# A count moved into the recurrence's bank, and chunk 13's second norm split around chunk 14's last up stages

## The chip, the cores and the metric

The kernel runs on one core of one Trainium2 chip. The metric is the device time of the whole program in microseconds (us). The engines are called PE (TensorE: matrix products), DVE (VectorE), ACT (ScalarE), POOL (GpSimd) and SP (SyncE, here only a queue that issues transfers). Each engine works through its own list of instructions; semaphores tie the lists together. PSUM is the memory into which PE writes its products; a tile of it that is needed again has first to be read by the engine that takes it over.

## The reference

The input x has 2 sequences of 4096 rows of 256 numbers. Two layers follow, each with a residual and a norm:

```
u = x @ W_in + b_in;  g = sigmoid(x @ W_gate + b_gate)
h_t = tanh(h_{t-1} @ A + u_t @ Bm)              # state of 64, step by step
y_t = g_t * (h_t @ C.T + u_t @ D.T) + (1 - g_t) * x_t
x = layernorm(x + (y @ W_out + b_out + x))
...
bw = mean(|w|, per row) * sign(w)               # for w1 (1024 x 256) and w2 (256 x 1024)
x = layernorm(x + gelu(x @ bw1.T + b1) @ bw2.T + b2)
```

## The kernel before

**The recurrence in segments.** Each sequence is cut into 64 segments of 64 steps, and all 128 segments run side by side. A run-in of 48 steps from a zero state gives each segment a guess of its first state. At the end `compare` (four DVE operations, L166 to L172) counts the states for which this guess agreed with what the segment before ended in, into `cnt`. `count` (L175) sums `cnt` over the partitions with a product by ones and copies the sum to `flag` (DVE, L178). All engines load the flag at L864; where some state was not met, a branch recomputes everything one segment after another. In the runs shown the branch is not taken.

**Chunks.** The 8192 rows are 16 chunks of 512 (`Chunk`, numbers 0 to 15; `end` is 15). A chunk's life is a row of small steps:

- `mix`, `mix_end`, `project(0)`, `project(1)`: the gated output and its product with W_out (PE, L400). At the end of `project(1)` DVE adds the residual (L411), which gives `x1`. `stats1`, `shift`, `norm` are the first layer norm.
- `turn` (for the chunks 0, 1 and 15) or `blocks` (the others): the transposed x1. It is split into a part `hi` rounded to the reduced type fp32r, and a rest `lo`, so that two products make up for one of full width. For `turn` these are L439 (ACT) and L441 (DVE), for `blocks` they are `split_hi` (ACT, L464) and `split_lo` (DVE, L468).
- `up(g)`, g = 0 to 3: two tiles of 128 hidden units. Each is four products of 128x512 (PE, L487) into a bank, and a GELU on ACT (L497) which reads the bank. After the second tile ACT rounds both to `hhi` (L506). `low(g)` is the rest `hlo` on DVE (L513).
- `down(g)`: sixteen products of 128x256 (PE, L529), hhi and hlo of two hidden tiles for four blocks of rows. At the end of `down(3)` DVE scales the sums out of PSUM (`scale`, L545).
- `rest` adds the bias b2 on POOL (L360), `add` the scaled sums to x1 on DVE (L551).
- `stats` is the second norm's statistics: on DVE `bn_stats` (L256), `bn_aggr` (L260) and the variance plus epsilon (L265), then its power -1/2 on POOL (L266). `store` follows: the shift `nm_b` on DVE (L271), four scalings on ACT (L279), and one transfer to the output, issued by SP (L566).

**Banks.** Up tiles, gates and, before the change, the count take PSUM tiles from a pool `p_1` of three banks with one tag, "h". `p_h` (L149) is a bank of its own, in which the recurrence's steps put their products. `mix`, `project` and `turn` share the pool `p_m`, the down sums have `p_2`; both have one tile.

**Order.** Nothing is reordered by a scheduler: the main part is one block with a manual schedule, and each engine gets its instructions in the order in which the program emits them. The loop over c at L778 staggers the chunks: turn c holds up(c), down(c - 1, 2) and down(c - 1, 3), then the end of chunk c - 1 (add, stats, store), down(c, 0) and down(c, 1), and the early steps of the chunks c + 1 and c + 2. The recurrence's steps are spread over the loop by costs and are over before turn 14. The change concerns turns 13 and 14; the numbers in what follows are chunk numbers, so low(14,1) is `low(1)` of chunk 14. In turn 14 the program emits before the change: up(14,0), low(13,3), the first norm of chunk 15, down(13,2), low(14,0), half of compare, up(14,1), down(13,3) with its scaling, turn(15), low(14,1), the other half of compare, add(13), stats(13), rest(15), up(14,2), low(14,2), store(13), down(14,0), up(14,3), down(14,1). After the loop follow the count, up(15,0), low(14,3), low(15,0), down(14,2), down(14,3), and the rest of chunks 14 and 15 (L843 to L860).

Of the kernel before, what the change touches and what calls it, by code (L numbers as in the profile page):

```python
# [8 lines left out]
FP = mybir.dt.float32  # L9
# [7 lines left out]
P = 128  # L17
# [6 lines left out]
N = 512  # L24
# [3 lines left out]
TB = N // P  # L28
# [9 lines left out]
def gated_recurrence_then_binary_ffn(  # L38
# [16 lines left out]
    nc = tc.nc  # L55
# [7 lines left out]
    p_1 = ctx.enter_context(tc.tile_pool(name="p_1", bufs=3, space=PSUM))  # L63
# [27 lines left out]
    ones = cp.tile([P, P], FP, name="ones")  # L91
    neg_half = cp.tile([P, TB], FP, name="neg_half")
    cnt = cp.tile([P, 2], FP, name="cnt")
    flag = cp.tile([1, 1], I32, name="flag")
# [54 lines left out]
    p_h = p_s.tile([P, W], FP, name="ps_s")  # L149
# [23 lines left out]
        yield  # L173

    def count():  # L175
        ps = p_1.tile([P, N], FP, tag="h", name="ps_cnt")
        nc.tensor.matmul(ps[0:1, 0:1], ones[:, 0:1], cnt[:, 0:1], start=True, stop=True)
        nc.vector.tensor_copy(flag, ps[0:1, 0:1])  # L178


    def load_weights():
# [148 lines left out]
    class Chunk:  # L330
# [218 lines left out]
        def add(self, blocks=range(TB), engine=nc.vector):  # L549
            cut = slice(blocks[0], blocks[-1] + 1)  # L550
            engine.tensor_tensor(  # L551
                self.x1[:, cut, :], self.x1[:, cut, :], self.o[:, cut, :], ALU.add
            )
            yield
# [88 lines left out]
    plan = [*range(L - WARM, L), *range(L)]  # L643
    done = 0
# [3 lines left out]
    def ready():  # L648
        return done < len(plan) and plan[done] // SPC in have_u

    def next_steps():
        nonlocal done
        steps(plan[done])
        done += 1
        if done == WARM:
            first_states()
        for i in range(3):
            if done == WARM + (i + 1) * SPC:
                ch[i].load_h()
        if waiting and not held:  # L660
            for what, args in waiting:
                what(*args)
            waiting.clear()
# [10 lines left out]
    def step():  # L674
        if ready():
            next_steps()

    def do(i, what, *args, pace=5600):
        if not 0 <= i < len(ch):
            return  # L680
        if what == "load":
            need = WARM + (ch[i].c + 1) * SPC
            while done < need:
                next_steps()
            ch[i].load_u()
            ch[i].load_h()
        elif what in ("load_n", "load_x", "load_gate_x"):
            getattr(ch[i], what)()
        else:
            emit(what, getattr(ch[i], what)(*args), pace)  # L690
# [7 lines left out]
    with tc.manual_schedule(engines={ET.PE, ET.Activation, ET.DVE, ET.Pool, ET.SP}):  # L698
        waiting = []
        for c in range(FIRST + 1, FIRST + 6):  # L700
            load_xT(c)
        idle_products(7)
        emit("u", u_of_chunks(FIRST), 1 << 30)
        since = 0
        pairs = [(5, 6), (7, 8), (9, 10), (11, 12), (13, 14), (), (1, 2)]
        loads = [[10, 11], [12, 13], [14, 15, 0], [1, 2], [3], [], []]
        for n, pair in enumerate(pairs):
            before = 2 if n == 0 else 1
            parts(before, EARLY)
            if pair:  # L710
                emit("", u_of_chunks(*pair))
                if pair == (13, 14):
                    emit("", u_of_chunks(15, 0))
                emit("u", [None], EARLY)
            for c in loads[n]:
                load_xT(c)
            if n == 0:
                load_weights()
            if n == 3:
                halve_weights()  # L720
            if n >= 5:
                load_xT(n + 3)
                ch[n - 4].load_n()
                if n == 5:
                    ch[0].load_u()
                else:
                    ch[0].load_n()
                    ch[1].load_u()
                    ch[2].load_u()
            for i in range(7 - before):  # L730
                if 1 <= n < 5 and i == 0:
                    load_w(n - 1)
                if 2 <= n < 6 and i == 3:
                    prepare_w(n - 2)
                parts(1 if (n, i) != (6, 5) else 0, EARLY)
        assert done >= WARM + SPC, done
        emit("u", u_of_chunks(3), EARLY)
        for i in range(4):
            ch[i].xt = x_tiles[i]
        ch[0].in_x = ch[1].in_x = True  # L740
        parts(1, 600)
        do(0, "mix", pace=850)
        do(0, "mix_end")
        held = True
        parts(2, 600)
        assert done >= WARM + 2 * SPC, done
        do(1, "mix", pace=850)
        do(1, "mix_end")
        held = False
        do(0, "project", 0, p_2, "o", pace=1700)  # L750
        do(0, "project", 1, pace=1700)
        do(0, "stats1")
        assert done >= WARM + 3 * SPC, done
        do(2, "mix", pace=1700)
        do(0, "shift")
        do(1, "project", 0, p_2, "o", pace=1700)
        do(0, "norm")
        do(1, "project", 1, pace=1700)
        do(1, "stats1")
        parts(1, 1700)  # L760
        while waiting:
            next_steps()
        waiting = None
        do(0, "turn", True)
        emit("", mean_w2())
        mixed = ch[2].mix_end()
        next(mixed)
        do(1, "norm", nc.vector)
        do(0, "rest")
        next(mixed)  # L770
        parts(2, 1700)
        for i in (4, 5):
            do(i, "load_x")
        end = len(ch) - 1
        parts_met = compare()
        since = -1 << 40
        late = gates(ch[10:], TB)
        for c in range(end):  # L778
            far = 0 < c < end - 1
            if far:  # L780
                do(c + 1, "shift")
                do(c + 1, "norm")
                do(c - 1, "low", 3)
                do(c + 1, "blocks")
            do(c, "up", 0)
            if c == end - 1:
                do(c - 1, "low", 3)
                do(c + 1, "shift")
                do(c + 1, "norm")
            step()  # L790
            do(c - 1, "down", 2)
            if c > 0:
                do(c + 2, "mix")
            do(c, "low", 0)
            mixed = ch[c + 2].mix_end() if 0 < c < end - 1 else iter(())
            next(mixed, None)
            if c == end - 1:
                assert done == len(plan), done
                next(parts_met)
                next(parts_met)  # L800
            do(c + 3, "load")
            do(c + 6, "load_x")
            if c % 2 == 0:
                do(10 + c // 2, "load_gate_x")
            do(c, "up", 1)
            step()
            do(c - 1, "down", 3)
            next(mixed, None)

            def add():  # L810
                do(c - 1, "add")
                do(c - 1, "stats")

            if 1 <= c <= 12:
                add()
                emit("gate", (next(late, None) for _ in range(KD)))
            if not far:
                do(c + 1, "turn")
            do(c, "low", 1)
            if c == end - 1:  # L820
                assert done == len(plan), done
                next(parts_met)
                next(parts_met)
            if not 1 <= c <= 12:
                add()
            do(c + 1, "rest")
            do(c, "up", 2)
            step()
            if far:
                do(c + 1, "split_hi")  # L830
            do(c, "low", 2)
            do(c - 1, "store", range(TB), nc.scalar)
            do(c + 3, "load_n")
            do(c, "down", 0)
            do(c + 2, "project", 0)
            do(c + 2, "project", 1)
            if far:
                do(c + 1, "split_lo")
            do(c + 2, "stats1")
            do(c, "up", 3)  # L840
            step()
            do(c, "down", 1)
        count()  # L843
        do(end, "up", 0)
        do(end - 1, "low", 3)
        do(end, "low", 0)
        do(end - 1, "down", 2)
        do(end - 1, "down", 3)
        do(end, "up", 1)
        do(end - 1, "add")  # L850
        do(end - 1, "stats")
        do(end, "low", 1)
        do(end, "up", 2)
        do(end, "low", 2)
        do(end, "down", 0, True)
        do(end, "up", 3, True)
        do(end - 1, "store", range(TB), nc.scalar)
        do(end, "low", 3, True)
        do(end, "down", 1)
        do(end, "down_end")  # L860
# [64 lines left out]
```

## Time and profile before

| what | value |
|---|---|
| median of 3 runs | 445.03 us (444.57 to 445.47) |
| time of the profiled execution | 445.99 us |
| span of its instructions | 444.1 us |
| mean granted PE clock in it | 0.985 of full speed |
| PE busy | 428.2 us |
| DVE, ACT, POOL busy | 332.6, 285.5, 153.3 us |
| HBM read, written | 31.43 MB, 8.39 MB |

All times in the text are counted from the start of the profiled span. In a timeline row the columns are start, length in us, engine, line of the kernel, operation, output<-input, shape and count; a bracket gives the idle time of the engine before the row and what ended it. A row of several instructions gives the length from the first start to the last end. In a row of waits the three numbers are total us, times and the longest. PEclk is the granted clock of PE; in the page's row of 40 slices it stands in tenths and 9 means 0.9 or more.

### The profile page before, as it was taken

The numbers are of one execution on the slowest core, as the hardware profiler recorded it, in microseconds if no ns is written. First come the engines' busy times: TensorE is split into PE (matmuls) and PEld (weight loads), VectorE is DVE, ScalarE is ACT, GpSimd is POOL, SyncE is SP. The second block draws the span as 40 slices with busy tenths as digits, with TensorE's granted clock in tenths as the row PEclk, the third lists the DMA queues.
The fourth block names the chain that finished last, engine by engine and source line by source line (L and its number), as shares of the span: only waits on it lengthen the run. The fifth ranks groups of instructions, "written<-read, shape, count | busy, mean of one in ns | idle before, by whom it ended". The sixth has DMA issues, their size and how long they took to land.

```text
span 444.1 us, 6819 instructions
## 1 busy us (share of the span) xinstructions
PE 428.2 (96%) x2402; PEld 346.8 (78%) x2402; DVE 332.6 (75%) x569; ACT 285.5 (64%) x480; POOL 153.3 (35%) x176
## 2 busy tenths in 40 slices
PE   8999999999999999999999999999999999998792
PEld 5665767788888888888888888888887888887781
DVE  0245927986879797969696979797979797977274
ACT  2443452577585958595868676867776768585681
POOL 1000040654342345243523452346252446351213
PEclk9999999999999999999999999999999999999697
DMA  8977614400242524262426251625251323210102
GB/s 299 305 272 261 245 35 131 154 1 7 63 149 57 206 57 154 50 211 55 159 48 216 46 168 43 217 49 169 44 170 42 125 45 121 46 52 0 47 1 100
DMA packets 31479, 51.34 MB, mean 116 GB/s; under 512 B 5328, under 2 KB 19664, under 8 KB 31440
## 3 DMA queue, kind: packets, MB, share of 16 engines
q1 hardware_dynamic: 30864, 50.48, 35.5%
q8 instruction: 21, 0.34, 0.3%
q10 hardware_dynamic: 576, 0.37, 0.3%
q14 instruction: 18, 0.15, 0.1%
HBM read 31.43 MB, written 8.39 MB: 90 GB/s over the span
## 4 chain that ended last, share of the span: by engine, by line
PE 84%; DVE 6%; ACT 4%; DMA 1%; POOL 1%; issue 1%; SPq 0%; POOLq 0%; DVEq 0%
PE ps_h L487 23%; PE ps_o L529 23%; PE ps_g L314 12%; PE ps_z L400 11%; PE ps_y L375 6%; PE ps_s L157 6%; PE ps_u L131 3%; ACT xn L279 2%; DMA xt<-in_xT 1%; ACT h L497 1%; DVE hlo L513 1%; POOL rs_b L266 1%; DVE bs_b L256 1%; ACT hhi L506 1%; DVE xlo L441 1%
## 5 line engine op out<-in xcount | busy, mean ns | idle before, releaser
L529 PE MATMUL ps_o<-sg,hhi 128*128 128x256 f32 x496 | 123.2, 288 | 0.0
L529 PE MATMUL ps_o<-sg,hlo 128*128 128x256 f32 x496 | 119.6, 281 | 0.1
L497 ACT ACTIVATE h<-ps_h,bias_c,al 128x512 f32<-128x512 f32 x128 | 95.2, 771 | 19.4 <-PE ps_h L487 16.1
L487 PE MATMUL ps_h<-xhi,sg 128*128 128x512 f32 x256 | 93.4, 446 | 4.4 <-DVE flag L178 2.9
L529 PEld LDWEIGHTS ps_o<-sg,hhi 128*128 128x128 f32 x496 | 95.0, 192 | 1.0 <-DVE o L545 0.2
L529 PEld LDWEIGHTS ps_o<-sg,hlo 128*128 128x128 f32 x496 | 94.8, 191 | 1.1 <-DVE hlo L513 0.3
L513 DVE TENSOR_TENSOR hlo<-h,hhi 128x1024 fp32r<-128x1024 f32 (+1 forms) x65 | 80.2, 1251 | 9.0 <-ACT hhi L506 9.0
L360 POOL TENSOR_TENSOR xn<-xn,bo_r 128x256 f32<-128x256 f32 x64 | 52.8, 856 | 90.2 <-DMA xn<-in_x 78.7
L487 PE MATMUL ps_h<-xlo,sg 128*128 128x512 f32 x256 | 80.5, 395 | 0.9 <-DVE xlo L468 0.8
L266 POOL TENSOR_TENSOR rs_b<-rs_b,neg_half 128x4 f32<-128x4 f32 (+1 forms) x17 | 29.0, 1703 | 125.8 <-DVE rs_b L265 125.7
L506 ACT CAST hhi<-h 128x1024 fp32r<-128x1024 f32 (+1 forms) x65 | 67.4, 1039 | 2.0
L314 PE MATMUL ps_g<-xt,w_gate 128*128 128x384 f32 (+3 forms) x208 | 66.2, 430 | 0.2 <-DMA w_gate<-in_W_gate 0.2
L487 PEld LDWEIGHTS ps_h<-xhi,sg 128*128 128x128 f32 x256 | 46.6, 190 | 23.1 <-issue 11.7
L158 ACT ACTIVATE st<-ps_s 64x128 f32<-64x128 f32 x112 | 29.9, 267 | 45.9 <-PE ps_s L157 45.5
L487 PEld LDWEIGHTS ps_h<-xlo,sg 128*128 128x128 f32 x256 | 48.3, 189 | 12.7 <-DVE xlo L468 1.2
L157 PEld LDWEIGHTS ps_s<-st,wab 128*128 128x128 f32 x224 | 38.5, 189 | 21.6 <-ACT st L158 9.6
L360 POOL TENSOR_TENSOR xn<-xn,b_r 128x256 f32<-128x256 f32 x64 | 52.3, 848 | 1.1 <-PE ps_t L431 1.1
L400 PE MATMUL ps_z<-w_out,tg 128*128 128x256 f32 x224 | 50.6, 379 | 0.0
L400 PEld LDWEIGHTS ps_z<-w_out,tg 128*128 128x128 f32 x224 | 41.4, 190 | 5.1
L157 PE MATMUL ps_s<-st,wab 128*128 128x128 f32 x224 | 43.8, 277 | 0.1
L279 ACT ACTIVATE xn<-xn,nm_a,rs_a 128x256 f32<-128x256 f32 x60 | 31.2, 591 | 14.4 <-DVE nm_a L271 14.4
L279 ACT ACTIVATE xn<-xn,nm_b,rs_b 128x256 f32<-128x256 f32 x62 | 32.3, 591 | 10.4 <-DVE nm_b L271 10.4
(79 smaller groups left out, 464.6 us busy)
## 6 DMA issues: line engine op xcount, KB each, us to landing
xt<-in_xT SPq DMA_DIRECT2D x35, 512.0 KB, 4.7
xn<-in_x SPq DMA_DIRECT2D x16, 512.0 KB, 3.3
out_y<-xn SPq DMA_DIRECT2D x15, 512.0 KB, 2.6
xlo<-xb SPq DMA_DIRECT2D x208, 32.0 KB, 1.9
hu<-st SPq DMA_DIRECT2D x32, 128.0 KB, 2.3
w1t<-in_w1T SPq DMA_DIRECT2D x2, 512.0 KB, 4.9
w1n<-in_w SPq DMA_DIRECT2D x2, 512.0 KB, 6.7
w2t<-in_w2T SPq DMA_DIRECT2D x2, 512.0 KB, 5.7
```

The costliest lines, as they stand in the source:

```text
L157: nc.tensor.matmul(p_h, ab, st[:, j].rearrange("p b k -> p (b k)"), start=True, stop=True)
L158: nc.scalar.activation(h_of[:, j + 1].rearrange("p b k -> p (b k)"), p_h[TOP, :], AF.Tanh)
L266: nc.gpsimd.tensor_tensor(rs, rs, neg_half[:, cut], ALU.pow)
L279: nc.scalar.activation(r, r, AF.Identity, bias=self.sh[:, i : i + 1], scale=rs)
L314: nc.tensor.matmul(ps[:, cut], w_gate[:, k, bass.ts(m, P)], xt_[:, k, cut], start=k == 0 and i == 0, stop=k == KD - 1, skip_group_check=True,)
L360: nc.gpsimd.tensor_tensor(r[:, i, :], r[:, i, :], row, ALU.add)
L400: nc.tensor.matmul(self.ps_z[:, i, :], self.y[:, k, bass.ts(i, P)], w_out[:, k, :], start=k == 0, stop=k == KD - 1,)
L487: nc.tensor.matmul(ps, sg1[:, k, bass.ts(j, P)], part[:, k, :], start=n == 0, stop=n == 2 * KD - 1,)
L497: nc.scalar.activation(to, ps.rearrange("p (a i c) -> p a i c", a=P // 32, c=32) if self.far else ps, AF.Gelu, bias=b1_c[:, j : j + 1], sc ...
L506: nc.scalar.copy(hi[:, part, :], h[:, part, :])
L513: nc.vector.tensor_sub(lo[:, i, :], h[:, i, :], hi[:, i, :].bitcast(FP))
L529: nc.tensor.matmul(ps[:, i, :], part[:, j % 2, bass.ts(tb, P)], sg2[:, j, :], start=j == 0 and part is self.h[j // 2][0] and first, stop=j ...
```

## The change

In `count` the product of the count goes into the recurrence's bank `p_h`, and no tile of the pool is taken. In turn 14 (c = end - 1) add(13) moves ahead of turn(15), right behind the scaling; stats(13) comes behind low(14,1), ahead of the second half of compare, which was ahead of it; store(13), with its shift, its four scalings and its transfer, moves from behind low(14,2) to behind up(14,3). In turn 13 (c = end - 2) split_lo(14) moves from behind project(15,1) to between project(15,0) and project(15,1). For all other turns the new conditions give the old order. An assertion of the program's construction goes.

```
     def count():
-        ps = p_1.tile([P, N], FP, tag="h", name="ps_cnt")
-        nc.tensor.matmul(ps[0:1, 0:1], ones[:, 0:1], cnt[:, 0:1], start=True, stop=True)
-        nc.vector.tensor_copy(flag, ps[0:1, 0:1])
+        nc.tensor.matmul(p_h[0:1, 0:1], ones[:, 0:1], cnt[:, 0:1], start=True, stop=True)
+        nc.vector.tensor_copy(flag, p_h[0:1, 0:1])
...
-            def add():
+            if c <= 12 or c == end - 1:
                 do(c - 1, "add")
+            if c <= 12:
                 do(c - 1, "stats")
-
             if 1 <= c <= 12:
-                add()
                 emit("gate", (next(late, None) for _ in range(KD)))
             if not far:
                 do(c + 1, "turn")
             do(c, "low", 1)
+            if c == end - 2:
+                do(c - 1, "add")
+            if c > 12:
+                do(c - 1, "stats")
             if c == end - 1:
-                assert done == len(plan), done
                 next(parts_met)
                 next(parts_met)
-            if not 1 <= c <= 12:
-                add()
             do(c + 1, "rest")
             do(c, "up", 2)
             step()
             if far:
                 do(c + 1, "split_hi")
             do(c, "low", 2)
-            do(c - 1, "store", range(TB), nc.scalar)
+            if c < end - 1:
+                do(c - 1, "store", range(TB), nc.scalar)
             do(c + 3, "load_n")
             do(c, "down", 0)
             do(c + 2, "project", 0)
+            if c == end - 2:
+                do(c + 1, "split_lo")
             do(c + 2, "project", 1)
-            if far:
+            if far and c < end - 2:
                 do(c + 1, "split_lo")
             do(c + 2, "stats1")
             do(c, "up", 3)
+            if c == end - 1:
+                do(c - 1, "store", range(TB), nc.scalar)
             step()
             do(c, "down", 1)
         count()
```

More of the change, by code (lines that the diff above doesn't have):

```diff
@@ L175, in count @@
     def count():
-        ps = p_1.tile([P, N], FP, tag="h", name="ps_cnt")
-        nc.tensor.matmul(ps[0:1, 0:1], ones[:, 0:1], cnt[:, 0:1], start=True, stop=True)
-        nc.vector.tensor_copy(flag, ps[0:1, 0:1])
+        nc.tensor.matmul(p_h[0:1, 0:1], ones[:, 0:1], cnt[:, 0:1], start=True, stop=True)
+        nc.vector.tensor_copy(flag, p_h[0:1, 0:1])
     def load_weights():
@@ L808, in gated_recurrence_then_binary_ffn @@
             next(mixed, None)
-            def add():
+            if c <= 12 or c == end - 1:
                 do(c - 1, "add")
+            if c <= 12:
                 do(c - 1, "stats")
             if 1 <= c <= 12:
-                add()
                 emit("gate", (next(late, None) for _ in range(KD)))
@@ L819, in gated_recurrence_then_binary_ffn @@
             do(c, "low", 1)
+            if c == end - 2:
+                do(c - 1, "add")
+            if c > 12:
+                do(c - 1, "stats")
             if c == end - 1:
-                assert done == len(plan), done
                 next(parts_met)
                 next(parts_met)
-            if not 1 <= c <= 12:
-                add()
             do(c + 1, "rest")
@@ L831, in gated_recurrence_then_binary_ffn @@
             do(c, "low", 2)
-            do(c - 1, "store", range(TB), nc.scalar)
+            if c < end - 1:
+                do(c - 1, "store", range(TB), nc.scalar)
             do(c + 3, "load_n")
@@ L835, in gated_recurrence_then_binary_ffn @@
             do(c + 2, "project", 0)
+            if c == end - 2:
+                do(c + 1, "split_lo")
             do(c + 2, "project", 1)
-            if far:
+            if far and c < end - 2:
                 do(c + 1, "split_lo")
@@ L840, in gated_recurrence_then_binary_ffn @@
             do(c, "up", 3)
+            if c == end - 1:
+                do(c - 1, "store", range(TB), nc.scalar)
             step()
```

## The prediction

> **What bounds the kernel now.** I read the page first: the busy shares and the row of granted clock.
>
> ```profile
> PE 428.2 (96%) x2402; PEld 346.8 (78%) x2402; DVE 332.6 (75%) x569; ACT 285.5 (64%) x480; POOL 153.3 (35%) x176
> PEclk9999999999999999999999999999999999999697
> ...
> ```
>
> TensorE (PE) is busy 96% of the span, so only work or waiting on PE can move the end. Its clock is full except in two slices near the end; the slice marked 6 is 410.8 to 421.9 us (each is 11.1 us). Next I asked for the waits between 386 and 424 us (total us, times, longest) and for PE's order of work there (start, length, line, idle before).
>
> ```profile
> ACT xn L279 <- DVE nm_b L271: 6.4, 2, 6.2
> ...
> PE ps_h L487 <- DVE flag L178: 2.9, 1, 2.9
> ...
> PE ps_h L487 <- ACT h L497: 1.5, 1, 1.5
> PE ps_h L487 <- DVE xlo L468: 0.8, 1, 0.8
> ```
>
> ```profile
> 408.62 0.19 PE L177 MATMUL ps_cnt<-cnt,ones 128*1 128x1 f32 x2
> 411.73 0.73 PE L487 MATMUL ps_h<-xhi,sg 128*128 128x512 f32 x2 [2.92 <-DVE flag L178]
> 412.30 0.63 PE L487 MATMUL ps_h<-xlo,sg 128*128 128x512 f32 x2
> 414.44 1.22 PE L487 MATMUL ps_h<-xhi,sg 128*128 128x512 f32 x2 [1.51 <-ACT h L497]
> ```
>
> PE does the 1x1 product of the count at 408.62, then stands for 2.92 us: the next product, tile 0 of chunk 15's first up stage, needs the bank that the count holds until VectorE (DVE) copies the flag. It then stands 1.51 us for a bank that ScalarE (ACT) has not read. Third, what holds DVE and ACT.
>
> ```profile
> 405.78 1.21 DVE L551 TENSOR_TENSOR xn<-xn,o 128x1024 f32<-128x1024 f32 x1
> 407.02 1.41 DVE L256 BATCH_NORM_STATS2 bs_b<-xn 128x6 f32<-128x256 f32 x4
> ...
> 410.94 0.68 DVE L271 SCALAR_TENSOR_TENSOR nm_b<-mv_b,rs_b 128x4 f32<-128x4 f32 x1 [0.90 <-POOL rs_b L266]
> 411.54 0.14 DVE L178 CAST flag<-ps_cnt 1x1 int32<-1x1 f32 x1
> ```
>
> ```profile
> 411.65 2.08 ACT L279 ACTIVATE xn<-xn,nm_b,rs_b 128x256 f32<-128x256 f32 x4 [6.18 <-DVE nm_b L271]
> 413.63 1.42 ACT L497 ACTIVATE h<-ps_h,bias_c,al 128x512 f32<-128x512 f32 x2
> ```
>
> Chunk 13's second norm is one chain: addition, statistics, the power on GpSimd (POOL), shift nm_b, four scalings on ACT. Both PE waits hang on it. The flag's copy stands behind nm_b on DVE; chunk 14's last GELUs, whose products ended near 406.9, stand behind the scalings on ACT. Fourth, the clock in short windows (length, PE busy, clock, DMA).
>
> ```profile
> 412.00:413.00 1.00, 0.93 (x4) 1.00 0.00 0
> 413.00:414.00 1.00, 0.00 (x0) 0.84 0.00 0
> 414.00:415.00 1.00, 0.56 (x1) 0.50 0.43 172
> 419.00:420.00 1.00, 1.00 (x7) 0.50 0.00 0
> 420.00:421.00 1.00, 1.00 (x8) 0.75 0.00 0
> 421.00:422.00 1.00, 1.00 (x11) 1.00 0.00 0
> ```
>
> The clock halves during the standstill and stays so until about 420.4; down products start every 0.213 us there, not every 0.115.
>
> **What the Trainium skill says.** "TensorE: Matmul & The Clock Gate", Part 1: the gate grants half clock after an idle window of about 3.4 us and the full one after as long a busy one; the window runs freely. The trace agrees: 2.92 and 1.51 us of standing between 408.8 and 414.4, only 1.2 us of work between them, then 0.50 for some 6.7 us. The same part says that ACT and DVE are strict first-in, first-out. The trace agrees: GELUs ready at 406.9 run at 413.63. "SBUF — State Buffer", Who interferes with whom: a DVE operation with two SBUF inputs and a POOL operation that reads SBUF lock each other out. The trace fits: L468 takes 1.42 us beside POOL's additions, L513 between 0.68 and 1.78, L271 0.68 directly behind POOL but 0.16 elsewhere.
>
> **The change, part by part.** I follow the queues again in the new order, with the old durations.
>
> *Chunk 13's turn: split_lo ahead of the second half of project.* DVE now runs L468 (1.42) before L411 (1.21). Chunk 14's hi half is ready at 390.60 and DVE free at 390.77, so xlo is ready at 392.2, not 393.24. PE asks for it at 392.35 (two products after 391.88), so the 0.79 us wait goes. But the next tile needs the bank that ACT reads from 392.79 to 393.55; it starts there, against 393.88 before. Gain **0.3 us**, the rest a new bank wait. L411 ends at 393.4; its statistics slip by 0.1 us, hidden, since ACT takes chunk 15's first norm only at 397.63.
>
> *Addition 13 behind its scaling.* DVE scales at 400.5 to 401.7 and then stands 1.32 us for ACT's xhi. The addition (1.21) fills that: ends 402.95, L441 can start at 403.06 as before. Free; without that cover it would cost 1.2 us on DVE.
>
> *Statistics 13 behind low(14,1), compare after them.* low(14,1) still ends at 405.42. Statistics from 405.35 take 1.9: variance ready 407.23 (was 408.91), POOL's power (1.85) ends 409.25, nm_b 409.3 to 409.95. The compare's two operations (0.5) end at 407.7; the count's product needs them and PE comes there at 408.3, so 0.6 us of slack where there were 2.7. low(14,2) ends at 408.85 (was 410.04); PE wants it at 410.4.
>
> *Norm and store 13 behind up(14,3).* ACT finishes hhi(14,2) at 405.47, goes straight on with the GELUs (405.7 to 407.4) and the cast (to 408.45), then the four scalings at 410.0 to 412.1. Queued behind these now are the GELUs of up(15,0), at 412.1 to 413.5 with their cast to 414.6. The first who wants them is tile 1 of up(15,1), which reuses that bank at 415.0: 2.2 us of slack. The store's one DMA on SP moves from after the old scalings (413.7) to after the new (412.1); only chunk 14's store follows on that queue, 20 us later. The flag's copy and low(14,3) stand behind nm_b on DVE: 410.1 and 410.1 to 411.3 (to 411.9 with L513's longest, 1.78); PE wants low(14,3) at 412.3.
>
> *Count in the recurrence's bank.* That bank's last tanh is long over (the steps all ended before), and nothing of the straight path uses it again. Tile 0 of up(15,0) then takes the third rotating bank, free since 404.4, tile 1 the bank of the GELU that ends at 406.5. PE runs through.
>
> *The sum.* From the last product of down(14,1) (next slot 408.53) to the first of up(15,1) (421.97) pass 13.44 us. What has to run there: count 0.2, eight up products at 0.233 = 1.86, 32 down products at 0.1155 = 3.70, together 5.76. Gain 7.68: 2.92 + 1.51 of standing, 2.9 of half clock (the 32 down products take 416.32 to 421.97, 5.65 us against 3.70; the four up products before them 1.88 against 0.93), and the rest, 0.35, at the restarts. With the 0.3 above: **8.0 us** at up(15,1), which starts near 414.0.
>
> *What is late next.* Behind that point the old tail runs on, shifted, but DVE takes low(15,0) only at 414.6 (it waits for that cast), so chunk 14's scaling runs 415.8 to 417.0, 1.4 us later against the shifted frame (PE wants its bank at 417.8). Addition and statistics follow to 420.1, low(15,1) to 421.3; PE wants it at 421.5. low(15,2) to 422.5 (wanted 423.6). low(15,3) waits for ACT as before. So the tail keeps the 8.0 with 0.2 us to spare at low(15,1); I take off 0.2 for that. Net **-7.8 us**.
>
> The profiled execution took 445.99 us (span 444.1 and 1.9 around it): 438.2. The runs' median, 445.03, is 0.96 lower; with the same difference 437.2.
>
> **The rivals.** *(B) DVE is late in the tail.* Slack is 0.6 us at the compare and 0.2 at low(15,1), and POOL's lock can add 0.5 to an operation. For: the tail's DVE chain from 414.6 to 422.5 has no gap. Against: only single operations meet POOL. It would cost 1 to 3 us: about 439.2.
>
> *(C) The clock gives nothing.* The page has the window run freely, so the timed runs may have paid less half clock than the profile, or the gate closes once more after the changed stage. Then only the waits go: 2.92 + 1.51 + 0.3 = 4.7, so 440.3. Against: the three times lie within 0.9 us, and the profile only 0.96 above their median, where 2.9 would be seen.
>
> *(D) It does not do what it says.* If tile 0 of up(15,0) gets a bank still unread, or PE stands at the count for cnt behind the statistics on DVE, the wait is only renamed. Then GELUs or statistics would have to be 3 us later than worked out: about 445.
>
> *(E) Slower.* The delay of DVE in the tail is long, not short: chunk 13's scalings hold back the GELUs of up(15,0), these hold back low(15,0), and all of chunk 14's scaling and second norm stand behind that on DVE. If low(15,1) came 6 us late (nm_b 13 ready only near 416), PE would stand 5.8 us near 421.5, longer than the page's window, so the gate would close again and cost the same 2.9 as before: 437.2 + 5.8 + 2.9 = 445.9. It decides where PE stands more than about 5.8 us. Against: nm_b would have to be later than it is now, although the work ahead of it on DVE shrinks.
>
> **How the numbers follow.** Forecast A (436.4 to 438.4) 0.70; B 0.13; C 0.10; D 0.03; E 0.04. Within 0.2% (about what a measurement of this kernel can tell from no change) lies D alone. The range reaches from half a microsecond below A, L271 at 0.16 and a full recovery, up to C: 436.2 to 440.5, leaving out D, E and the worst of B and C. Faster 0.93, same 0.03, slower 0.04.
>
> **What would show it.** Right: no wait of L487 on flag, clock 1.00 from 396 to 432, GELUs of up(14,3) at 405.7, ACT's scalings of chunk 13 near 410, up(15,1) near 414, xlo's wait replaced by some 0.7 for a bank. Wrong: a PE wait on low(15,1) or on cnt above 0.5 us, or a clock below 1.00 after 396.

## The result, and the profile after

The changed kernel takes **437.69 us** (median of 4 runs, 437.48 to 437.96), the kernel before 445.16 (4 runs, 444.57 to 445.47). The ratio is 0.9834, with a 95% interval from 0.9817 to 0.9851: 7.5 us or 1.7% faster. The profiled execution took 437.67 us with a span of 435.9 us.

`count` is one line shorter now, so lines behind L177 count one less up to the loop: up is L486, down L528, the norm's shift L270. First the page of the kernel after, busy shares and granted clock:

```profile
PE 425.5 (98%) x2402; PEld 344.3 (79%) x2402; DVE 332.4 (76%) x569; ACT 286.0 (66%) x480; POOL 155.8 (36%) x176
PEclk9999999999999999999999999999999999999997
...
```

The slice with the 6 is gone; the last 7 is the time after the last product. The waits of the kernel after between 386 and 436 us (total us, times, longest), and PE's timeline there:

```profile
ACT xn L278 <- DVE nm_b L270: 4.5, 3, 3.5
...
PE ps_h L486 <- ACT h L496: 0.3, 1, 0.3
PEld ps_o L528 <- DVE hlo L512: 0.3, 1, 0.3
```

```profile
392.54 0.74 PE L486 MATMUL ps_h<-xlo,sg 128*128 128x512 f32 x2
393.57 0.73 PE L486 MATMUL ps_h<-xhi,sg 128*128 128x512 f32 x2 [0.28 <-ACT h L496]
...
408.43 0.19 PE L176 MATMUL ps_s<-cnt,ones 128*1 128x1 f32 x2
408.55 0.74 PE L486 MATMUL ps_h<-xhi,sg 128*128 128x512 f32 x2
...
414.27 0.63 PE L486 MATMUL ps_h<-xhi,sg 128*128 128x512 f32 x2
```

The count's product is followed at once by up(15,0), and up(15,1) starts at 414.27, where it started at 421.97 before: 7.70 us of the 8.2 by which the span shrank. The last product of the program ends 7.7 us earlier too. The other half microsecond lies behind the last DVE instruction, where the final store ends: 4.2 us to the end of the span, against 4.7 before. This last stretch lies anywhere between 4.0 and 4.9 us in the profiles shown here, so the half microsecond can't be put down to the change. ACT and DVE of the kernel after:

```profile
405.78 1.70 ACT L496 ACTIVATE h<-ps_h,bias_c,al 128x512 f32<-128x512 f32 x2 [0.15 <-PE ps_h L486]
407.51 1.05 ACT L505 CAST hhi<-h 128x1024 fp32r<-128x1024 f32 x1
409.05 2.08 ACT L278 ACTIVATE xn<-xn,nm_b,rs_b 128x256 f32<-128x256 f32 x4 [0.48 <-DVE nm_b L270]
411.03 1.43 ACT L496 ACTIVATE h<-ps_h,bias_c,al 128x512 f32<-128x512 f32 x2
```

```profile
401.57 1.23 DVE L550 TENSOR_TENSOR xn<-xn,o 128x1024 f32<-128x1024 f32 x1
403.22 1.23 DVE L440 TENSOR_TENSOR xlo<-ps_t,xhi 128x1024 fp32r<-128x1024 f32 x1 [0.42 <-ACT xhi L438]
...
408.87 0.15 DVE L270 SCALAR_TENSOR_TENSOR nm_b<-mv_b,rs_b 128x4 f32<-128x4 f32 x1
```

Chunk 14's last GELUs run at 405.78 instead of 413.63 and no longer stand behind the scalings. The addition lies in the gap ahead of L440. The shift nm_b starts at 408.87, against 410.94 before.

### The profile page after: what moved, and what is told of

The parts are those of the page before. It is cut to its first block, busy times and chain, and to the rows that moved or that the text cites. A ratio compares the mean times of both kernels' runs of the same rounds, so it can differ in the third digit from the quotient of the medians.

```text
span 435.9 us, 6818 instructions
## 1 busy us (share of the span) xinstructions
PE 425.5 (98%) x2402; PEld 344.3 (79%) x2402; DVE 332.4 (76%) x569; ACT 286.0 (66%) x480; POOL 155.8 (36%) x176
## 4 chain that ended last, share of the span: by engine, by line
PE 89%; DVE 5%; ACT 2%; DMA 1%; issue 1%; POOL 1%; SPq 0%; POOLq 0%; DVEq 0%
PE ps_h L486 25%; PE ps_o L528 25%; PE ps_g L313 12%; PE ps_z L399 11%; PE ps_y L374 6%; PE ps_s L157 6%; PE ps_u L131 3%; DMA xt<-in_xT 1%; DVE hlo L512 1%; ACT xn L278 1%; POOL rs_b L265 1%; PE ps_t L430 1%; DVE bs_b L255 1%; DVE d L381 1%; ACT h L496 1%
## 5 line engine op out<-in xcount | busy, mean ns | idle before, releaser
L528 PE MATMUL ps_o<-sg,hhi 128*128 128x256 f32 x496 | 121.4, 286 | 0.0
L528 PE MATMUL ps_o<-sg,hlo 128*128 128x256 f32 x496 | 117.9, 279 | 0.1
L528 PEld LDWEIGHTS ps_o<-sg,hhi 128*128 128x128 f32 x496 | 93.5, 189 | 1.1 <-DVE o L544 0.3
L528 PEld LDWEIGHTS ps_o<-sg,hlo 128*128 128x128 f32 x496 | 93.5, 188 | 1.1 <-DVE hlo L512 0.3
L486 PE MATMUL ps_h<-xhi,sg 128*128 128x512 f32 x256 | 92.9, 444 | 0.3 <-ACT h L496 0.3
L359 POOL TENSOR_TENSOR xn<-xn,bo_r 128x256 f32<-128x256 f32 x64 | 54.7, 888 | 88.6 <-DMA xn<-in_x 78.4
L512 DVE TENSOR_TENSOR hlo<-h,hhi 128x1024 fp32r<-128x1024 f32 (+1 forms) x65 | 79.5, 1240 | 5.0 <-ACT hhi L505 5.0
L486 PE MATMUL ps_h<-xlo,sg 128*128 128x512 f32 x256 | 80.1, 394 | 0.2
L265 POOL TENSOR_TENSOR rs_b<-rs_b,neg_half 128x4 f32<-128x4 f32 (+1 forms) x17 | 28.1, 1655 | 115.1 <-DVE rs_b L264 105.0
L486 PEld LDWEIGHTS ps_h<-xhi,sg 128*128 128x128 f32 x256 | 46.5, 189 | 18.9 <-issue 11.7
L486 PEld LDWEIGHTS ps_h<-xlo,sg 128*128 128x128 f32 x256 | 48.0, 188 | 11.9 <-DVE xlo L440 0.7
L265 POOL TENSOR_TENSOR rs_a<-rs_a,neg_half 128x4 f32<-128x4 f32 x16 | 17.2, 1072 | 65.0 <-DVE rs_a L264 63.0
```

What stands on the lines that cost most here:

```text
L265: nc.gpsimd.tensor_tensor(rs, rs, neg_half[:, cut], ALU.pow)
L359: nc.gpsimd.tensor_tensor(r[:, i, :], r[:, i, :], row, ALU.add)
L486: nc.tensor.matmul(ps, sg1[:, k, bass.ts(j, P)], part[:, k, :], start=n == 0, stop=n == 2 * KD - 1,)
L512: nc.vector.tensor_sub(lo[:, i, :], h[:, i, :], hi[:, i, :].bitcast(FP))
L528: nc.tensor.matmul(ps[:, i, :], part[:, j % 2, bass.ts(tb, P)], sg2[:, j, :], start=j == 0 and part is self.h[j // 2][0] and first, stop=j ...
```

## The experiments

Each of the three groups was timed beside the kernel before on one chip; a ratio is to the runs of that kernel in the same group. Of the first four runs (kernel before: 445.02, 18 runs from 443.96 to 446.54) three do parts of the change alone and one fills the standstill.

**The count's bank alone.**

```
-        ps = p_1.tile([P, N], FP, tag="h", name="ps_cnt")
-        nc.tensor.matmul(ps[0:1, 0:1], ones[:, 0:1], cnt[:, 0:1], start=True, stop=True)
-        nc.vector.tensor_copy(flag, ps[0:1, 0:1])
+        nc.tensor.matmul(p_h[0:1, 0:1], ones[:, 0:1], cnt[:, 0:1], start=True, stop=True)
+        nc.vector.tensor_copy(flag, p_h[0:1, 0:1])
```

> Only the count's bank is changed. My theory: the wait on the flag goes, but the second tile of up(15,0) still needs the bank whose GELU stands behind chunk 13's scalings on ACT (read to about 414.4 us), so PE stands there some 4.9 us instead of 2.9 + 1.5 us, and the clock still halves: 445.0 us, within 0.5 of before. Rival (the bank alone is the gain): at least the 2.9 us of the flag's wait go, 442.2 us or less.

Measured: 444.91 us (12 runs), ratio 0.9995 (0.998 to 1.001). PE's timeline of this kernel:

```profile
408.57 0.19 PE L176 MATMUL ps_s<-cnt,ones 128*1 128x1 f32 x2
414.42 1.22 PE L486 MATMUL ps_h<-xhi,sg 128*128 128x512 f32 x2 [4.51 <-ACT h L496]
```

The wait for the flag is gone: the first tile of up(15,0) starts at 408.69, right behind the count. PE stands 4.51 us for the GELU instead. The second tile starts at 414.42, where it started at 414.44 before. Two waits in a row ended with the same chain, and taking the first away gave its time to the second.

**The late norm and store alone.**

```
-            do(c - 1, "store", range(TB), nc.scalar)
+            if c < end - 1:
+                do(c - 1, "store", range(TB), nc.scalar)
...
             do(c, "up", 3)
+            if c == end - 1:
+                do(c - 1, "store", range(TB), nc.scalar)
```

> Only chunk 13's second norm and store move behind up(14,3); the count keeps its bank of the pool. My theory: the 1.5 us wait for the bank goes, the wait for the flag stays (copy behind nm_b near 411.5 us), up to 2.9 us[...]; if the clock stays full, 4.4 us are gained: 440.8 us. Rival (a wait of 2.9 us closes the gate too): only 1.5 us, 443.7 us.

Measured: 439.80 us, ratio 0.9887 (0.987 to 0.9903), a microsecond better than my better case. The GELUs of up(14,3) run at 406.01, where they ran at 413.63 before. The copy of the flag is as late as ever (411.56), but PE does not wait for it. The first product of up(15,0) starts right behind the count, with no idle time in front of it:

```profile
406.01 1.70 ACT L497 ACTIVATE h<-ps_h,bias_c,al 128x512 f32<-128x512 f32 x2 [0.55 <-PE ps_h L487]
...
408.66 0.19 PE L177 MATMUL ps_cnt<-cnt,ones 128*1 128x1 f32 x2
408.77 0.74 PE L487 MATMUL ps_h<-xhi,sg 128*128 128x512 f32 x2
...
411.56 0.14 DVE L178 CAST flag<-ps_cnt 1x1 int32<-1x1 f32 x1
...
422.91 0.38 PE L529 MATMUL ps_o<-sg,hlo 128*128 128x256 f32 x1 [0.25 <-DVE hlo L513]
...
425.69 0.39 PE L529 MATMUL ps_o<-sg,hlo 128*128 128x256 f32 x1 [0.22 <-DVE hlo L513]
```

(The last two rows are the only ones of PE with idle time behind the count.) With the GELUs early, the tile of up(15,0) can't be in the count's bank, since that is read only at 411.56. The granted clock is 1.00 from 404 to 428 us. So this one edit removes both waits and the half clock.

**PE kept busy, all waits left in.** The added products fill the standstill; their result is not read.

```
         count()
+        idle_products(14)
         do(end, "up", 0)
```

> The kernel before with 14 products of ones by ones (128x128, result never read) behind the count, about as long as the 2.9 us that PE stands there; all waits stay. My theory: PE counts as busy, the clock stays full and the 2.9 us of half clock are gained: 442.3 us. Rival (the half clock costs nothing, only the waits do): 445.2 us or, with the added products in the way, more.

Measured: 443.34 us (7 runs, 443.19 to 443.81), ratio 0.9969 (0.9958 to 0.9981): by this interval 0.8 to 1.9 us gained by adding work. PE's windows of this kernel (length, busy, clock, DMA):

```profile
408.00:410.00 2.00, 2.00 (x19) 1.00 0.00 0
410.00:412.00 2.00, 2.00 (x20) 1.00 0.00 0
412.00:414.00 2.00, 1.04 (x5) 1.00 0.00 0
414.00:416.00 2.00, 1.55 (x9) 1.00 0.65 262
416.00:418.00 2.00, 2.00 (x19) 1.00 0.00 0
```

The clock stays full although 1.41 us of waiting for the GELU are still there. The second tile of up(15,0) starts at 414.45, as before, but up(15,1) already at 419.33, against 421.97, and the last product at 432.45, against 435.08. So in the profile of the kernel before the half clock costs 2.6 us; between the medians it is 1.7. The profiled execution of before (445.99) is one of its long ones, with a mean granted clock of 0.985. Of the 36 runs of this kernel in the three groups four have this clock, and they took 445.54 to 446.54; the other 32 have 0.987 to 0.989 and took 443.96 to 446.12. That fits a half clock that lasts longer in some executions than in others.

**Bank and late norm together.** Both edits above.

> The count's bank and the late norm and store together; addition, statistics and split_lo stay where they were. My theory: both PE waits go and the clock stays full, but nm_b comes only at 411 to 411.6 us, so low(14,3), the GELUs of up(15,0) and with them chunk 14's scaling and low(15,1) come 1.5 us later than in the kernel after; PE stands 0.2 us at low(14,3) and about 1 us in the tail: 439.0 us. Rival (the early addition and statistics bring nothing, the two other edits are all): 438.0 us, which is the kernel after without the 0.3 us of split_lo.

Measured: 439.57 us, ratio 0.9884 (0.9865 to 0.9903), the same as the late norm alone. The rival is out: without the early addition and statistics (and the early split_lo, which a run below finds worth next to nothing) 1.7 us of the gain are missing. PE's rows with idle time show a part of it:

```profile
413.32 0.38 PE L528 MATMUL ps_o<-sg,hlo 128*128 128x256 f32 x1 [0.61 <-DVE hlo L512]
...
425.57 0.39 PE L528 MATMUL ps_o<-sg,hlo 128*128 128x256 f32 x1 [0.23 <-DVE hlo L512]
```

low(14,3) stands behind nm_b on DVE, which comes at 410.81 here. Half of the loss comes there: up(15,1) starts at 415.14, 0.87 us later than in the kernel after. The other half comes in the tail: chunk 14's scaling starts at 417.21 instead of 414.72, and the last product is 1.72 us late (429.11 against 427.39).

The second group (kernel before: 445.06) undoes or adds single steps in the changed kernel.

> The changed kernel again, as the measure for the runs beside it: 437.7 us.

Measured: 437.92 us (437.62 to 438.10), ratio 0.9839 (0.9826 to 0.9853).

**split_lo back.**

```
             do(c + 2, "project", 0)
-            if c == end - 2:
-                do(c + 1, "split_lo")
             do(c + 2, "project", 1)
-            if far and c < end - 2:
+            if far:
                 do(c + 1, "split_lo")
```

> The changed kernel with split_lo(14) back behind project(15,1). My theory: xlo comes about 1 us later, PE stands 0.8 us for it but no longer for the bank: 0.3 us more than the changed kernel, 438.0 us. Rival (a wait there is absorbed before turn(15), where PE would stand for the norm anyhow): no difference, 437.7 us.

Measured: 437.85 us, ratio 0.9841 (0.9827 to 0.9854): no difference. In the traces it makes up(14,0)'s second tile 0.3 us earlier (393.62 against 393.89) and up(15,1) 0.2 (414.32 against 414.49); both spans are 436.1. A fifth of a microsecond is below what the times can tell. The gain on the spot is not certain either: in the last run below, which keeps split_lo early, chunk 14's input landed later (ACT's cast of it starts at 390.05, against 389.62), and PE stood 0.78 us for xlo again.

**Chunk 12's norm late as well.**

```
-            if c < end - 1:
+            if c < end - 2:
                 do(c - 1, "store", range(TB), nc.scalar)
...
-            if c == end - 1:
+            if c >= end - 2:
                 do(c - 1, "store", range(TB), nc.scalar)
```

> The changed kernel with chunk 12's norm and store also behind its up stage, up(13,3). My theory: the GELUs of up(13,3) then run before the scalings, up(14,0) finds its bank free, PE gains the 0.28 us and what follows until turn(15), where chunk 15's norm stops it 0.2 us ahead of now: 0.2 us less, 437.5 us. Rival (the scalings only push ACT's later GELUs back and the wait comes again at up(14,1)): no change or up to 0.5 us more.

Measured: 439.44 us, ratio 0.9873 (0.9858 to 0.9888), 1.5 us slower than the changed kernel. My theory fell. DVE of this kernel:

```profile
393.97 1.41 DVE L255 BATCH_NORM_STATS2 bs_a<-xn 128x6 f32<-128x256 f32 x4
395.29 0.37 DVE L259 BATCH_NORM_AGGREGATE mv_a<-bs_a 128x2 f32<-128x6 f32 x4
395.69 0.17 DVE L264 TENSOR_SCALAR rs_a<-mv_a 128x4 f32<-128x4 f32 x1
395.77 0.16 DVE L270 SCALAR_TENSOR_TENSOR nm_b<-mv_b,rs_b 128x4 f32<-128x4 f32 x1
```

The shift is part of the store. Moved, it fell behind split_lo, the residual and all of stats1 on DVE (at 395.77, where it stood at 390.03); ACT waited 2.53 us for it, and up(14,1) stood 1.43 us for a bank.

**up(15,3) ahead of down(15,0).**

```
-        do(end, "down", 0, True)
         do(end, "up", 3, True)
+        do(end, "down", 0, True)
```

> The changed kernel with up(15,3) ahead of down(15,0) at the end. My theory: the last wait on PE, 0.33 us for low(15,3) in the last down products, goes, since GELUs, cast and low(15,3) get the time of the 16 products of down(15,0): 0.35 us less, 437.3 us. Rival (a bank or the third hhi buffer holds it up just as long): no difference or up to 0.5 us more.

Measured: 437.31 us (437.01 to 437.70), ratio 0.9828 (0.9815 to 0.9842). The last wait for low(15,3) is no longer in the trace, and the span is 435.5.

The third group (kernel before: 444.96) follows up.

**The count back in the pool, all else changed.** The bank's edit, reversed.

> The changed kernel with the count back in a bank of the pool. My theory by now: with the late norm the bank edit is worth nothing, since up(15,0) finds another bank read long before, as it did when only the norm was late: 437.9 us, within 0.3 of the changed kernel. Rival (what the prediction said: the tile takes the count's bank and waits for the flag, now copied near 409.0 us): 0.5 us of standing, 438.4 us.

Measured: 437.77 us, ratio 0.9836 (0.9822 to 0.9851). The bank is worth nothing beside the late norm. The first tile of up(15,0) starts at 408.78, right behind the count (408.66), and the flag is copied only at 409.21, so the tile is in another bank again.

**The addition back behind low(14,1).**

```
-            if c <= 12 or c == end - 1:
+            if c <= 12:
                 do(c - 1, "add")
...
-            if c == end - 2:
+            if c > 12:
                 do(c - 1, "add")
```

> The changed kernel with chunk 13's addition back behind low(14,1); statistics stay ahead of compare. DVE's chain then comes 1.2 us later. My theory: low(14,3) and low(15,1) have 1 to 1.5 us to spare in the changed kernel, so most of it is absorbed: 0.0 to 0.4 us more, 438.1 us. Rival (the chain is on the path throughout, since undoing addition and statistics together cost 1.7 us): 1.2 us more, 439.1 us.

Measured: 438.46 us, ratio 0.9853 (0.9836 to 0.987): 0.5 to 0.8 us more than the changed kernel in the two groups that have it (437.69 and 437.92), and 0.7 more than the run before, which has the pool's bank and all else of the change. That lies between my theory and the rival. The last product comes 0.6 us later than in the kernel after (428.00 against 427.39). The cost is in a place that neither named. PE's timeline:

```profile
408.95 0.19 PE L176 MATMUL ps_s<-cnt,ones 128*1 128x1 f32 x2 [0.62 <-DVE cnt L172]
```

PE stood for the second half of compare, which now follows the addition and the statistics on DVE.

**Only chunk 12's scalings late,** on top of the version with up(15,3) first.

```
-            if engine is nc.scalar:
+            if engine is nc.scalar and not shifted:
                 self.st2.shift(blocks)
...
-            if c < end - 1:
+            if c < end - 2:
                 do(c - 1, "store", range(TB), nc.scalar)
+            if c == end - 2:
+                ch[c - 1].st2.shift(range(TB))
...
-            if c == end - 1:
-                do(c - 1, "store", range(TB), nc.scalar)
+            if c >= end - 2:
+                do(c - 1, "store", range(TB), nc.scalar, nc.sync, c == end - 2)
```

> The version with up(15,3) ahead of down(15,0), and in addition chunk 12's four scalings and store behind up(13,3), its shift on DVE where it was. My theory: the loss of 1.6 us with the whole norm moved came from the shift, which fell behind three DVE steps; with the shift in place the GELUs of up(13,3) free the bank in time, PE gains some 0.25 us until turn(15): 437.1 us. Rival (ACT is full there and the order of its work makes no difference, or the later GELUs of up(14,0) suffer): 437.3 to 438 us.

Measured: 437.39 us (437.30 to 438.18), ratio 0.983 (0.9815 to 0.9846). The loss of the whole norm moved is gone, as it must be if the shift was its cause, and PE has no idle row of its own left between 388 us and the last products. As to a gain, compare the same version without this step, in the same group:

> The version with up(15,3) ahead of down(15,0) again, beside the others: 437.3 us.

Measured: 437.72 us (437.46 to 438.43), ratio 0.9838 (0.9822 to 0.9853). The two versions with up(15,3) first are the fastest in their groups, by 0.05 to 0.6 us, with overlapping intervals. Their spans (435.5 to 435.7 against 435.9 to 436.1) speak for some 0.4 us; the times leave it open.

## Why the prediction was right, and where it was not

**The sum over PE's queue held.** 7.68 us were forecast between the last product of down(14,1) and up(15,1), plus 0.3 ahead of it. The trace has 7.70 in all (414.27; forecast 414.0): 5.93 us pass in that stretch where 5.76 were forecast, and 0.2 of the 0.3 are left when PE gets there. No other wait took the place of the two, and the clock is 1.00 from 396 us to the last product.

**The share of the parts did not.** The prediction put the end of the flag's wait, 2.92 us, down to the count's new bank. The runs give that edit nothing, alone (0.9995) or as the last to be undone (437.77). The late norm alone is worth 5.2 us: it removes both waits and the half clock. That step failed in its assumption that the tile of up(15,0) sits in the count's bank whatever the order; with the GELUs early it does not. How a bank is chosen when the program is built no run shows, so why stays open.

**Addition and statistics were needed, for more than was said.** The prediction called the addition free and put the worth of the early chain into slack. Together they are worth 1.7 us (439.57 against 437.92, with split_lo's share in it). The addition alone shows about 0.6 of it, and just where the prediction had worked out 0.6 us of slack, at the count's product. The rest, about 1.1 us, belongs to the statistics ahead of compare, or to both together; no run separates them.

**Slack in the tail was underrated.** nm_b was forecast at 409.3 to 409.95 and ran at 408.87 to 409.02. POOL's power took 1.01 us and not 1.85, so that nm_b had only low(14,2) ahead of it on DVE to wait for, and the shift took 0.15, not 0.68. low(15,1) ended at 420.25, not 421.3, so the 0.2 us taken off for it were not needed.

**split_lo** brought its 0.3 us on the spot, though L467 took 1.71 us instead of the 1.42 used, and next to nothing at the end. As xlo came later than forecast, the new wait for a bank is 0.28 us and not some 0.7.

**The median** was forecast at 437.2 and is 437.69. The profile's own time was forecast at 438.2 and is 437.67; most of this half microsecond is the one at the final store, which was not in the forecast. The step that carried the 0.96 us between profile and median over to the new kernel failed: the new kernel's profiled time and its median are the same. The likely cause is a long half clock in the profiled execution of before, as the granted clocks above suggest; it went with the half clock. The forecast took 7.8 us off profile and median alike, though the half clock cost the median run about a microsecond less. The profile's 7.7 us at the last product would then leave some 6.8 us for the median; 7.5 were measured (6.6 to 8.1 by the interval of the ratio). So the nearness of the median's forecast is in part luck.

**Two readings were loose.** "L513 between 0.68 and 1.78" mixes two sizes: 0.68 is the tile of 128x512 at the very end, the tiles of 128x1024 take 1.21 us or more. And L271 does not take 0.68 us because it is directly behind POOL. In the profile of before it took 0.68 to 0.71 in the sixteen cases in which an addition on POOL (L360) had begun just ahead of it, and 0.16 or 0.17 in the twelve in which POOL's power had just ended and no addition followed. In the kernel after, the addition began at 408.50 while an L512 was running, and the shift at 408.87 took 0.15.

**The rivals.** C, that the clock gives nothing, is refuted by the filled kernel, though its first ground was sound: the timed runs pay less than that profile (1.7 us between the medians against 2.6). B, a late DVE chain, is what the kernel becomes without the early addition and statistics. D and E did not come. The trace of the first edit alone is D's picture: a wait renamed, and no time gained.

## What to carry to other kernels

When two waits in a row end with the same chain of another engine, ask what the first wait would turn into; the edit that moves the chain takes both, and an edit for one of them may be worth nothing. Before a step is moved, go through each queue that its instructions use: the same store was worth 5 us when moved in one turn and cost 1.5 in the turn before, for one small DVE instruction in it. A standstill of TensorE may cost more than its length, so look at the granted clock behind it.

## What was not expected of the hardware

The standstill that halved the clock need not be in one piece: 2.92 and 1.51 us with 1.2 us of products between them did it. The clock fell at about 413.7 us (worked out from its mean of 0.84 between 413 and 414), so 0.8 us into the second of them. 4.51 us in one piece, with the count's bank alone, did it too, and 1.41 us by itself left the clock full. So where the prediction says that the trace agrees with an idle window of 3.4 us, it agrees in kind; how long a standstill has to be no run here shows. The full clock came back about 6 us after PE had taken up work again (414.44 to some 420.5).

The kernel before, with its standstill, scattered over 2.6 us in 18 runs (443.96 to 446.54), and over 1.1 and 1.7 us in the 9 runs of each of the other two groups. The versions with the full clock scattered over 0.5 to 1.1 us, in 4 to 7 runs each. That fits the free-running window of the Trainium skill's "TensorE: Matmul & The Clock Gate", Part 1, but no run takes it apart.

POOL's power of 128x4 took 1.85 us where it began 0.24 us behind an L513 of two SBUF inputs (409.06 after 408.82), and 1.01 where it began 0.21 us ahead of one (407.52 before 407.73). It is so throughout: in the profiles of before and after, the 30 powers of this size that began while an L513 (L512 after) was running took 1.50 to 1.92 us, the 32 others 1.01 to 1.03. This fits the lock that the Trainium skill's "SBUF — State Buffer", Who interferes with whom, describes: who comes first keeps the port. The other way round the trace does not show it for the power: the L512 at 407.73, which began while a power ran, took its usual 1.21 us. No run took it apart by itself.
